# A byte limit on the transfers under way, and a weight folding in 14 TensorE groups instead of 26

## The chip, the cores and the metric

The kernel runs on one core of a Trainium2 chip. The metric is the time of one execution in device microseconds (us), the median of three runs. Five engines work side by side, each through its own instructions in order: TensorE (PE; its weight loads are shown as PEld), VectorE (DVE), ScalarE (ACT), GpSimd (POOL) and SyncE (SP). SP issues nearly all transfers of this kernel. An engine waits on semaphores for what another engine or a transfer has to deliver.

## The reference

There are 32 graphs of 512 nodes with 128 features each, `x` (32, 512, 128), and one symmetric 0/1 adjacency matrix per graph, `adj` (32, 512, 512). Four layers follow each other. Each normalises `x` over the features, takes the positive part `h`, and adds the layer's result to `x`:

```
h = jnp.maximum(_layernorm(x, axis=-1), 0.0); x = x + layer(h, adj, ...)
```

- Layer 0 is masked attention: q, k and v are each relu(h W + b), then a softmax of q k over the neighbours, times v.
- Layer 1 is a graph convolution whose weight matrix, one per graph, comes from an LSTM of 128 steps. It runs over a convolution of the last 128 nodes. The steps depend on each other, all 32 graphs advance together.
- Layer 2 is four sublayers, with 1, 1, 2 and 3 blocks of 128 input features. Each is

```
src_agg = einsum('bjv,bij->biv', nodes @ ws + bs, _l2norm(adj, 2))
dst_agg = einsum('bjv,bji->biv', nodes @ wd + bd, _l2norm(adj, 1))
upd = concatenate([src_agg, nodes @ wn + bn, dst_agg], axis=2)
out = tanh(upd @ wu + bu)
```

- Layer 3 is a graph convolution with a PReLU.

Because `adj` is symmetric, the two aggregations of a sublayer of layer 2 are with the same matrix. So `wu` can be multiplied into `ws`, `wd` and `wn` beforehand: `ws wu[0] + wd wu[2]` is one matrix that is applied before the aggregation, `wn wu[1]` another that is applied to the nodes themselves. The biases fold in the same way: `bs wu[0] + bd wu[2]` becomes a row, `bn wu[1] + bu` a column. This is the "folding" that the change edits. It is done once per call, for the four sublayers.

## The kernel before

**Recorded operations and a planner.** The function `symmetric` doesn't issue instructions. It records operations by the helpers `PE`, `ACT`, `DVE`, `POOL` and `DMA` (L853), each with an estimated duration, a rank, and the tiles that it reads and writes. One operation is one group: the instructions inside it stay together on the engine. `Plan.run` (L599) then simulates the engines with these estimates, takes what can start first and among those the lower rank, and gives out buffers (PSUM banks under the tag "mm", SBUF tiles under tags such as "ar", "gs", "x"). The result is one order per engine, which is issued at L754. Transfers stand in SP's order as the planner put them. A transfer has `gap`, the time that the planner expects from the end of its issue to its landing: 2.0 us by default, 3.8 (`LANDED`) for the loads of pass 2. The planner also charges `SWITCH` when PE changes between operations marked `tiled` (quarters of 32 columns) and others.

**Stages.** `pass_1` (L1116) runs over the 32 graphs: it loads `x` (f_x), normalises, makes queries, keys and values, stores keys and values (f_dkq, f_dv) to a scratch area in HBM, completes layer 0 for the last 128 nodes and makes the LSTM's inputs f_seq. `lstm` (L1210) makes the 128 steps, whose operations have the smallest ranks and so go first: matmuls f_z (L1224), then tanh on ACT (f_th), and products on DVE, ending in the write of f_seq (L1269) that the next step's f_z waits for. Between the steps of the LSTM the engines work on `pass_2` (L1279, ranks 20,000 and above). Per graph it loads f_h2 (192 KB), f_k2 (256), the adjacency matrix f_a (four tiles of 256, L1293), f_v2 (258), f_x2 (192 and 64). It then finishes layer 0 with the tiled matmuls f_pq, f_s and f_po (L1306, L1315, L1324), stores f_dx (L1335), and, for the first 22 graphs, squares the adjacency on ACT (f_ar, L1363), forms the first aggregation of layer 1 (f_pg, L1409, not tiled) and stores it (f_dgT, L1351). `rest` (L1423, ranks 30,000 and above) does the remaining layers graph by graph after the LSTM.

**The folding.** `fold(i, FOLD)` (L982) is called for the four sublayers behind graphs 4, 7, 10 and 13 of pass 2. It uses these groups on PE. Per block of 128 input features: three transposes of weights (f_wT, L998) and three matmuls (f_pw, L1005 to L1007), 7 blocks in all. Per sublayer: three transposes of bias rows (f_bT, L1014), two matmuls of them with `wu` (f_pb, L1021, L1022), and one matmul for the column (f_pc, L1026). That is 2 x 7 + 3 x 4 = 26. The bias rows come as three loads f_rowb (L986), each of one row of 512 bytes copied into all 128 partitions (64 KB). The weights come as one load f_w2 (L988) of 384, 384, 576 or 768 KB. Each f_wT and f_bT is copied to SBUF by ACT, and each f_pw by ACT into f_wf; DVE writes the folded bias row (L942) and the folded column (f_bcol).

Of the kernel before, what the change touches and what calls it, by code (L numbers as in the profile page):

```python
# [8 lines left out]
FP = mybir.dt.float32  # L9
# [4 lines left out]
P = 128  # L14
# [3 lines left out]
L2_CHUNKS = (1, 1, 2, 3)  # L18
# [14 lines left out]
C_Q, C_K, C_N, C_U = 0, 1, 2, 6  # L33
N_C = 9
R_V, R_CONV, R_SD, R_U3, R_L3 = 0, 1, 2, 10, 11
# [453 lines left out]
W_F = [0, 1, 2, 4]  # L489
# [26 lines left out]


class Op:
    __slots__ = ("engines", "rank", "no", "deps", "cells", "waits", "ready", "end", "engine", "start", "next", "gap", "tiled", "patience")


class Plan:
# [22 lines left out]
    def __init__(self, bufs, fifo, banks):  # L545
        self.banks = banks
        self.last = float("inf")
        self.soon = 0.0
        self.spared = float("inf")
        self.left = 0  # L550
        self.sealed = 0
        self.kept = ("mm", "gs",)
        self.ops = []
        self.bufs = bufs
        self.made = {}
        self.fifo = {t: [] for t in fifo}
# [12 lines left out]
    def op(self, engines, rank, reads=(), writes=(), after=(), gap=0.0, tiled=False):  # L569

        o = Op()
        o.engines, o.rank, o.no, o.gap = engines, rank, len(self.ops), gap
        o.tiled = tiled
        o.patience = 0.15
        deps = set(after)
        cells = []
        for acc, is_write in [(a, False) for a in reads] + [(a, True) for a in writes]:
            c, part = acc if isinstance(acc, tuple) else (acc, None)
            if c not in cells:
                cells.append(c)  # L580
            for key, (ws, rs) in c.parts.items():
                if part is None or key is None or key == part:
                    deps.update(ws)
                    if is_write:
                        deps.update(rs)
            mine = c.parts.setdefault(part, ([], []))
            if is_write:
                c.parts[part] = ([o], [])
            else:
                mine[1].append(o)  # L590
        deps.discard(o)
        o.deps = list(deps)
        o.cells = [c for c in cells if c.pool is not None]
        for c in o.cells:
            c.left += 1
        self.ops.append(o)
        return o

    def run(self, tc, queues):  # L599
        import bisect  # L600
# [14 lines left out]
        for o in ops:  # L615
            if o.rank >= self.last:
                k, sub = divmod(o.rank - self.last, 10)
# [71 lines left out]
        tiled = False  # L689
        by_rank = sorted((o for o in ops if o.rank >= 10_000 and o not in apart), key=lambda o: -o.rank)  # L690
        while done < len(ops):
            best = None
            for e, cands in pools.items():
                first = None
                held = expected.get(e)
                for rank, no, o in cands:
                    r = room(o)
# [22 lines left out]
            s, e, o = best  # L720
# [6 lines left out]
            if e == "PE":  # L727
                tiled = o.tiled
# [22 lines left out]
            done += 1  # L751
        self.order = order
        order.sort(key=lambda o: (o.start, o.no))
        with tc.manual_schedule(engines=queues):  # L754
            for o in order:
                o.engines[o.engine][1]()


def symmetric(ctx, tc, x, adj, weights, cols, rows, lstm_b, prelu_a, out, fail):
# [12 lines left out]
    nc = tc.nc  # L772
# [13 lines left out]
    SOON = 9_950.0  # L786
    LANDED = 3.8
    STORED = 5.0
    PATIENCE = 0.9
# [5 lines left out]
    const = ctx.enter_context(tc.tile_pool(name="f_const", bufs=1))  # L795
# [9 lines left out]
    plan = Plan(BUFS, ("ar", "x", "inv", "n0", "n1", "n2", "n3", "a"), "mm")  # L805
# [24 lines left out]
    T_TR = 0.11  # L830
# [7 lines left out]
    def t_dma(kb):  # L838
        return 0.1 + kb / 315.0

    def PE(rank, t, fn, r=(), w=(), **k):
        return plan.op({"PE": (t, fn)}, rank, r, w, **k)

    def ACT(rank, t, fn, r=(), w=(), **k):
        return plan.op({"ACT": (t, fn)}, rank, r, w, **k)

    def DVE(rank, t, fn, r=(), w=(), **k):
        return plan.op({"DVE": (t, fn)}, rank, r, w, **k)
# [2 lines left out]
        return plan.op({"POOL": (t, fn)}, rank, r, w, **k)  # L851

    def DMA(rank, kb, fn, r=(), w=(), **k):  # L853
        return plan.op({"SP": (max(0.45, t_dma(kb)), fn)}, rank, r, w, gap=k.pop("gap", 2.0), **k)

    def turn_tiles(dst, src):

# [22 lines left out]
    ident = const.tile([P, P], FP, name="f_ident")  # L880
# [27 lines left out]
    folded = plan.fixed(wf)  # L908
    bcols = plan.fixed(bcol)
    HEAD, LAST = 10_000, 19_000  # L910

    def load(rank, kb, dst, src):
        c = plan.fixed(dst)
        DMA(rank, kb, lambda: nc.sync.dma_start(dst, src), [], [c])
        return c
# [7 lines left out]
    for j in range(P // TURN):  # L923
        part = bass.ts(j, TURN)
        DMA(HEAD + 100, 4, lambda part=part: nc.sync.dma_start(
            lb[part], lstm_b.rearrange("s q f -> (s q) f")[:, part].partition_broadcast(TURN)), [], [(w_lb, j)])
    w_lstm = load(HEAD + 100, 512, w[:, W_IH : W_SD[0], :], weights[:, W_IH : W_SD[0], :])
    w_last = load(LAST, 64, w_fc, weights[:, W_FC, :])
    w_alpha = load(LAST, 1, alpha, prelu_a.partition_broadcast(P))
    POOL(LAST, 0.2, lambda: nc.gpsimd.tensor_scalar_mul(minus_alpha, alpha, -1.0), [], [w_alpha])  # L930
# [10 lines left out]
    def bias_row(rank, k, row, r):  # L941
        DVE(rank, t_dve(P), lambda: nc.vector.tensor_copy(brow[:, k, :], row()), r, [(biases, k)])  # L942
# [38 lines left out]

    def fold(i, FOLD):  # L982
        o = W_SD[i]
        rowb = new("ar", (P, 3, P), f"f_rowb_{i}")
        for k, r in enumerate((R_SD + 2 * i, R_SD + 2 * i + 1, R_U3)):
            DMA(FOLD, 64, lambda k=k, r=r: nc.sync.dma_start(rowb.t[:, k, :], rows[r].partition_broadcast(P)), [], [(rowb, k)])  # L986
        w2 = new("ar", (P, W_U[i] + 3 - o, P), f"f_w2_{i}")
        DMA(FOLD, 64 * (W_U[i] + 3 - o), lambda: nc.sync.dma_start(w2.t, weights[:, o : W_U[i] + 3, :]), [], [w2])  # L988

        def wu(k):  # L990
            return w2.t[:, W_U[i] - o + k, :]

        for c in range(L2_CHUNKS[i]):
            tp = bank(f"f_wT_{i}_{c}", (P, 3, P), whole=False)

            def turn(tp=tp, c=c):
                for k, m in enumerate((W_SD[i] + 2 * c, W_SD[i] + 2 * c + 1, W_N[i] + c)):
                    nc.tensor.transpose(tp.t[:, k, :], w2.t[:, m - o, :], ident)  # L998
            PE(FOLD, 3 * T_TR, turn, [w2], [tp])
            wt = new("gs", (P, 3, P), f"f_wTs_{i}_{c}")  # L1000
            ACT(FOLD, 0.5, lambda tp=tp, wt=wt: nc.scalar.copy(wt.t, tp.t), [tp], [wt])
            pw = bank(f"f_pw_{i}_{c}", (P, 2, P), whole=False)

            def mults(wt=wt, pw=pw):
                nc.tensor.matmul(pw.t[:, 0, :], wt.t[:, 0, :], wu(0), start=True, stop=False)  # L1005
                nc.tensor.matmul(pw.t[:, 0, :], wt.t[:, 1, :], wu(2), start=False, stop=True)
                nc.tensor.matmul(pw.t[:, 1, :], wt.t[:, 2, :], wu(1), start=True, stop=True)  # L1007
            PE(FOLD, 3 * t_mm(P), mults, [wt, w2], [pw])
            ACT(FOLD, 0.4, lambda pw=pw, c=c: nc.scalar.copy(wf[:, W_F[i] + c, :, :], pw.t), [pw], [(folded, (i, c))])
        bt_ps = bank(f"f_bT_{i}", (P, 3, P), whole=False)  # L1010

        def turn_b():
            for k in range(3):
                nc.tensor.transpose(bt_ps.t[:, k, :], rowb.t[:, k, :], ident)  # L1014
        PE(FOLD, 3 * T_TR, turn_b, [rowb], [bt_ps])
        bt = new("gs", (P, 3, P), f"f_bTs_{i}")
        ACT(FOLD, 0.5, lambda: nc.scalar.copy(bt.t, bt_ps.t), [bt_ps], [bt])
        pb = bank(f"f_pb_{i}", (P, P), whole=False)

        def mult_b():  # L1020
            nc.tensor.matmul(pb.t, bt.t[:, 0, :], wu(0), start=True, stop=False)  # L1021
            nc.tensor.matmul(pb.t, bt.t[:, 1, :], wu(2), start=False, stop=True)  # L1022
        PE(FOLD, 2 * t_mm(P), mult_b, [bt, w2], [pb])
        bias_row(FOLD, i, lambda: pb.t, [pb])
        pc = bank(f"f_pc_{i}", (P, 2), whole=False)
        PE(FOLD, 0.2, lambda: nc.tensor.matmul(pc.t[:, 0:1], wu(1), colb[:, C_N + i : C_N + i + 1], start=True, stop=True),  # L1026
           [w2, w_cols], [pc])
        DVE(FOLD, 0.2, lambda: nc.vector.tensor_add(bcol[:, i : i + 1], pc.t[:, 0:1],
                                                    colb[:, C_U + i : C_U + i + 1] if i < 3 else bt.t[:, 2, 0:1]),
            [pc, bt], [(bcols, i)])  # L1030


    def ln_stats(rank, xc, tiles, name, at=0):
# [576 lines left out]
    end = lstm()  # L1610
# [5 lines left out]
        rest(b, k, end)  # L1616
    counted()
    E = mybir.EngineType
    plan.last, plan.spared, plan.soon = 30_000, 20_000, SOON
    plan.run(tc, {E.PE, E.Activation, E.DVE, E.Pool, E.SP})  # L1620
    return flag[0]

# [81 lines left out]
```

## Time and profile before

| what | value |
|---|---|
| time, median of 3 runs | 1311.23 us (1306.88 to 1315.88) |
| time of the profiled execution | 1314.59 us |
| its span, first to last instruction | 1312.7 us |
| mean granted TensorE clock | 0.994 |
| moved by transfers | 232.82 MB, mean 177 GB/s |
| f_bT: median of one matmul | 273 ns (12) |
| f_pw: median of one matmul | 377, 275 and 275 ns (14 each) |
| ACT copies f_bTs | 4, median 487 ns |
| SP issue of one f_rowb | 428 ns median (12) |

The profile is of one execution, on the core that ran. "Busy" of PE is from the start of a matmul to its modelled end, so matmuls overlap in it, and an fp32 matmul appears as two entries. A group's line names source line, engine, operation, and "out<-in" tiles. The chain of waits is the work that ended last, followed back from the end step by step to what released it; "issue" in it is time in which an engine waited for nothing that the profile shows. In the table of waits, the three numbers are us in total, how often, and the longest. In the windows, each engine has its busy us and its instruction count, and the last three columns are the granted clock, the busy share of the 16 DMA engines and GB/s.

### The profile page before, as it was taken

To read this page: it belongs to the slowest core of one execution; us is meant where nothing else is said; L and a number is where in the kernel's file an instruction comes from. 1 tells how busy PE (TensorE), PEld (TensorE's weight loads), DVE (VectorE), ACT (ScalarE), POOL (GpSimd) and SP (SyncE) were. 2 spreads that over 40 slices of the span, in tenths; PEclk is the share of its full clock that TensorE was granted. 3 is DMA by queue.
4 is the path that set the end of the run, shared out by engine and by line. 5 is a ranking of instruction groups with operands and counts; after the bars stand their busy time and mean duration, and the time that the engine had idled before them with its cause. 6 is when DMAs were issued, how large, how long until landed. Compare 5 with 4: busy or idle time off the path is not lost.

```text
span 1312.7 us, 32944 instructions
## 1 busy us (share of the span) xinstructions
PE 1272.8 (97%) x12097; PEld 979.3 (75%) x12097; DVE 988.7 (75%) x3274; ACT 834.8 (64%) x2093; POOL 393.3 (30%) x733
## 2 busy tenths in 40 slices
PE   9999999999899999899999999999999999999996
PEld 6888866666567777677878778787787877877774
DVE  7999878778779887677667677676776787787654
ACT  5666667667678654577466666666666666675433
POOL 5655532112213233432213213132131332332000
PEclk9999999999899999999999999999999999999999
DMA  8888888847757867899377776777766465773311
GB/s 264 271 279 271 277 275 252 263 155 240 233 149 251 265 187 168 201 201 218 93 150 163 159 165 152 151 164 160 161 153 143 91 137 139 142 169 65 53 28 36
DMA packets 301259, 232.82 MB, mean 177 GB/s; under 512 B 139680, under 2 KB 246688, under 8 KB 301088
## 3 DMA queue, kind: packets, MB, share of 16 engines
q1 hardware_dynamic: 284192, 213.84, 59.4%
q0 software_dynamic: 16896, 16.78, 8.2%
q8 instruction: 98, 1.61, 0.5%
q14 instruction: 73, 0.60, 0.2%
HBM read 136.98 MB, written 62.13 MB: 152 GB/s over the span
## 4 chain that ended last, share of the span: by engine, by line
PE 85%; DVE 5%; ACT 3%; POOL 2%; DMA 2%; issue 2%; SPq 0%; ACTq 0%; DVEq 0%; POOLq 0%
PE f_pa L1409 17%; PE f_pa L1524 14%; PE f_py L1513 14%; PE f_pg L1409 9%; PE f_po L1324 5%; PE f_s L1315 5%; PE f_z L1224 4%; PE f_p L1565 2%; PE f_pol L1174 2%; PE f_pk L1131 2%; PE f_pv L1147 2%; PE f_pl L1467 2%; PE f_sl L1164 2%; PE f_pd L1199 1%; PE f_pq L1306 1%
## 5 line engine op out<-in xcount | busy, mean ns | idle before, releaser
L1409 PE MATMUL f_pa<-f_ar,f_y 128*128 128x512 f32 x1024 | 295.0, 426 | 2.1 <-ACT f_y L1392 2.1
L1409 PEld LDWEIGHTS f_pa<-f_ar,f_y 128*128 128x128 f32 x1024 | 189.3, 188 | 72.3 <-issue 35.8
L1513 PE MATMUL f_py<-f_wf,f_n 128*128 128x128 f32 x1280 | 173.5, 275 | 0.0
L1513 PEld LDWEIGHTS f_py<-f_wf,f_n 128*128 128x128 f32 x1280 | 164.4, 192 | 10.0 <-issue 1.9
L1524 PE MATMUL f_pa<-f_n,f_wf 128*128 128x512 f32 x320 | 152.9, 593 | 0.1
L1528 ACT ACTIVATE f_n<-f_pa,f_bcol 128x512 f32<-128x512 f32 x128 | 88.2, 689 | 93.6 <-PE f_pa L1524 93.4
L1363 ACT ACTIVATE f_ar<-f_a 128x512 fp32r<-128x512 f32 x216 | 133.7, 622 | 7.1 <-DMA f_a<-in_adj_dram 3.7
L1392 ACT CAST f_y<-f_py 128x512 fp32r<-128x512 f32 x128 | 74.8, 585 | 93.8 <-PE f_py L1513 90.7
L1481 POOL DMA_DIRECT2D f_das<-f_ar x32 | 27.9, 873 | 341.5 <-ACT f_ar L1363 267.9
L1324 PE MATMUL f_po<-f_v,f_e 128*32 128x129 f32 x3072 | 107.0, 274 | 7.5 <-issue 7.4
L1520 DVE TENSOR_TENSOR f_pa<-f_pa,f_inv 128x512 f32<-128x512 f32 x128 | 86.8, 694 | 27.7 <-PE f_pa L1409 27.4
L1324 PEld LDWEIGHTS f_po<-f_v,f_e 128*32 128x32 f32 x3072 | 90.4, 110 | 21.8 <-issue 15.2
L1393 DVE TENSOR_TENSOR f_y<-f_py,f_y 128x512 fp32r<-128x512 f32 x128 | 87.6, 685 | 24.1 <-ACT f_y L1392 23.8
L1315 PE MATMUL f_s<-f_q,f_k 128*32 128x384 f32 x1024 | 103.3, 490 | 0.6 <-issue 0.6
L1224 PE MATMUL f_z<-f_w,f_seq 128*32 128x128 f32 x2040 | 85.1, 277 | 8.6 <-DVE f_seq L1269 4.3
L1524 PEld LDWEIGHTS f_pa<-f_n,f_wf 128*128 128x128 f32 x320 | 57.5, 190 | 47.1 <-issue 37.8
L1224 PEld LDWEIGHTS f_z<-f_w,f_seq 128*32 128x32 f32 x2040 | 54.5, 109 | 45.1 <-ACT f_e L1318 8.7
L1486 DVE SCALAR_TENSOR_TENSOR f_junk<-f_a,f_aT 128x1024 bf16<-128x1024 f32 x64 | 78.1, 1220 | 5.7 <-DMA f_aT<-f_das 4.7
L1409 PE MATMUL f_pg<-f_ar,f_xp_d 128*128 128x512 f32 x256 | 75.2, 417 | 0.5 <-DVE f_lw L870 0.3
L1058 ACT ACTIVATE f_xn_c<-f_x,f_sh_c,f_rs_c 128x128 f32<-128x128 f32 x138 | 58.0, 486 | 24.2 <-DVE f_sh_c L1066 24.1
L1318 ACT ACTIVATE f_e<-f_s 128x384 f32<-128x384 f32 x128 | 60.7, 485 | 19.8 <-PE f_s L1315 14.8
L1513 PE MATMUL f_py<-f_wf,f_T_c 128*128 128x128 f32 x448 | 72.9, 275 | 0.0
(202 smaller groups left out, 2734.9 us busy)
## 6 DMA issues: line engine op xcount, KB each, us to landing
f_a<-in_adj_dram SPq DMA_DIRECT2D x30, 1024.0 KB
f_a<-in_adj_dram SPq DMA_DIRECT2D x96, 256.0 KB
f_das<-f_ar POOLq DMA_DIRECT2D x32, 512.0 KB, 4.8
f_dkq<-f_kh SPq DMA_DIRECT2D x32, 448.0 KB
f_dv<-f_v SPq DMA_DIRECT2D x32, 258.0 KB
f_v<-f_dv SPq DMA_DIRECT2D x32, 258.0 KB
f_x<-in_x_dram SPq DMA_DIRECT2D x32, 256.0 KB
f_al<-in_adj_dram SPq DMA_DIRECT2D x32, 256.0 KB
```

Of the source, the lines that this page charges most:

```text
L1224: nc.tensor.matmul(z.t[part, k, :, :], h, w[:, m : m + 4, part], start=False, stop=True, skip_group_check=True)
L1315: PE(R, t_mm(NR), lambda s=s, j=j: quarters(lambda p: nc.tensor.matmul(s.t[p], keys.t[:, j * P + p.start : j * P + p.stop], q.t, start=Tru ...
L1324: PE(R, t_mm(P), lambda t=t, j=j: quarters(lambda p: nc.tensor.matmul(po.t[p, t, :], es[j].t[:, t * P + p.start : t * P + p.stop], v.t[:, ...
L1363: ACT(rank, 0.62, lambda t=t: nc.scalar.activation(ar.t[:, t, :], a.t[:, t, :], AF.Square, accum_out=deg.t[:, t : t + 1]), [(a, t)], [(ar, ...
L1392: ACT(rank, t_act(N), lambda: nc.scalar.copy(parts.t[:, :, 0, :], src.t), [src], [(parts, 0)])
L1393: DVE(rank, t_dve(N), lambda: nc.vector.tensor_sub(parts.t[:, :, 1, :], src.t, f32(parts.t[:, :, 0, :])), [src, (parts, 0)], [(parts, 1)])
L1409: nc.tensor.matmul(pg.t, parts.t[:, j, k, :], ar.t[:, j, :], start=(k == 0 and j == 0), stop=(k == 1 and j == NT - 1))
L1486: nc.vector.scalar_tensor_tensor(junk, flat(a.t[:, 2 * k : 2 * k + 2, :]), 1.0, flat(aT.t[:, 2 * k : 2 * k + 2, :]), OP.mult, OP.not_equal ...
L1513: nc.tensor.matmul(py.t[:, j, :], nodes[n].t[:, bass.ts(j, P)], wf[:, W_F[i] + c, 0, :], start=False, stop=(c == nch - 1), skip_group_chec ...
L1520: before = DVE(R, t_dve(N), lambda pa=pa: nc.vector.tensor_mul(pa.t, pa.t, inv_row.t), [inv_row], [pa])
L1524: nc.tensor.matmul(pa.t, wf[:, W_F[i] + c, 1, :], nodes[n].t, start=False, stop=(c == nch - 1), skip_group_check=True)
L1528: ACT(R, 0.57, lambda pa=pa, n=n, i=i: nc.scalar.activation(n.t, pa.t, AF.Tanh, bias=bcol[:, i : i + 1]), [pa], [n])
```

## The change

Two things are changed.

First, a limit. Each operation now has `kb`, the size that the helper `DMA` was given. When the orders are issued, `hold_back` looks back along SP's order. For an operation of a rank from 20,000 to below 30,000 it adds up its own size and those before it until the sum would exceed 768 KB, and makes it wait until the transfer at which that happens has landed. The planner's simulation doesn't know of it. Before, SP's transfers were limited only by the eight semaphores that they use in turn.

```
+    def hold_back(self, tc, flight, o):
+        if not self.spared <= o.rank < self.last:
+            return
+        kb = 0
+        for ins, more in reversed(flight):
+            if kb + more > self.in_flight:
+                tc.add_manual_dep(flight[-1][0], ins.name, mybir.DependencyInfo(
+                    mybir.DependencyClass.Sync, mybir.DependencyReason.DATA), reason="transfers under way")
+                return
+            kb += more
...
+        flight = []
         with tc.manual_schedule(engines=queues):
             for o in order:
-                o.engines[o.engine][1]()
+                made = o.engines[o.engine][1]()
+                if o.engine == "SP":
+                    flight.append((made.ins, o.kb))
+                    self.hold_back(tc, flight, o)
...
-    plan.last, plan.spared, plan.soon = 30_000, 20_000, SOON
+    plan.last, plan.spared, plan.soon, plan.in_flight = 30_000, 20_000, SOON, 768
```

Second, the folding. The bias rows are no longer loaded as rows and transposed. One load at the start, f_sd_col, brings the nine bias vectors as columns (128 partitions x 9), element by element. As a stationary operand, a column is repeated 128 times by a stride of zero. The two bias matmuls and the column's matmul write into the same PSUM bank as the last block's f_pw, in the same group. The groups are then 7 of transposes and 7 of products, 14. The planner may let the product groups wait (`patience` 0.9 in place of 0.15) where they would reach into the expected start of an LSTM operation.

```
+    sd_col = const.tile([P, R_U3 + 1 - R_SD], FP, name="f_sd_col")
+    sd_cols = load(HEAD + 100, 5, sd_col, rows[R_SD : R_U3 + 1].rearrange("r p -> p r"))
...
-        rowb = new("ar", (P, 3, P), f"f_rowb_{i}")
-        for k, r in enumerate((R_SD + 2 * i, R_SD + 2 * i + 1, R_U3)):
-            DMA(FOLD, 64, lambda k=k, r=r: nc.sync.dma_start(rowb.t[:, k, :], rows[r].partition_broadcast(P)), [], [(rowb, k)])
...
-        bt_ps = bank(f"f_bT_{i}", (P, 3, P), whole=False)
...
-        pb = bank(f"f_pb_{i}", (P, P), whole=False)
...
-        pc = bank(f"f_pc_{i}", (P, 2), whole=False)
...
+        def mult_b(pw):
+            for k in range(2):
+                nc.tensor.matmul(pw.t[:, 2, :], sd_col[:, 2 * i + k : 2 * i + k + 1].to_broadcast([P, P]), wu(2 * k), start=k == 0, stop=k == 1)
+            nc.tensor.matmul(pw.t[:, 3, 0:1], wu(1), colb[:, C_N + i : C_N + i + 1], start=True, stop=True)
+        for c in range(nch):
+            last = c == nch - 1
+            pw = bank(f"f_pw_{i}_{c}", (P, 4, P), whole=False)
+
+            def both(c=c, pw=pw, last=last):
+                mults(c, pw)
+                if last:
+                    mult_b(pw)
+            PE(FOLD, (6 if last else 3) * t_mm(P), both, [wts[c], w2] + ([sd_cols, w_cols] if last else []), [pw]).patience = PATIENCE
+            ACT(FOLD, 0.4, lambda pw=pw, c=c: nc.scalar.copy(wf[:, W_F[i] + c, :, :], pw.t[:, 0:2, :]), [pw], [(folded, (i, c))])
+        bias_row(FOLD, i, lambda: pw.t[:, 2, :], [pw])
```

Since the planner works from the recorded operations, the orders of all engines are computed anew.

More of the change, by code (lines that the diff above doesn't have):

```diff
@@ L518 @@
 class Op:
-    __slots__ = ("engines", "rank", "no", "deps", "cells", "waits", "ready", "end", "engine", "start", "next", "gap", "tiled", "patience")
+    __slots__ = ("engines", "rank", "no", "deps", "cells", "waits", "ready", "end", "engine", "start", "next", "gap", "tiled", "patience", "kb")
 class Plan:
@@ L548, in __init__ @@
         self.soon = 0.0
+        self.in_flight = float("inf")
         self.spared = float("inf")
@@ L574, in op @@
         o.patience = 0.15
+        o.kb = 0
         deps = set(after)
@@ L853, in DMA @@
     def DMA(rank, kb, fn, r=(), w=(), **k):
-        return plan.op({"SP": (max(0.45, t_dma(kb)), fn)}, rank, r, w, gap=k.pop("gap", 2.0), **k)
+        o = plan.op({"SP": (max(0.45, t_dma(kb)), fn)}, rank, r, w, gap=k.pop("gap", 2.0), **k)
+        o.kb = kb
+        return o
     def turn_tiles(dst, src):
@@ L983, in fold @@
         o = W_SD[i]
-        rowb = new("ar", (P, 3, P), f"f_rowb_{i}")
-        for k, r in enumerate((R_SD + 2 * i, R_SD + 2 * i + 1, R_U3)):
-            DMA(FOLD, 64, lambda k=k, r=r: nc.sync.dma_start(rowb.t[:, k, :], rows[r].partition_broadcast(P)), [], [(rowb, k)])
+        nch = L2_CHUNKS[i]
         w2 = new("ar", (P, W_U[i] + 3 - o, P), f"f_w2_{i}")
@@ L991, in wu @@
             return w2.t[:, W_U[i] - o + k, :]
-        for c in range(L2_CHUNKS[i]):
+        wts = []
+        for c in range(nch):
             tp = bank(f"f_wT_{i}_{c}", (P, 3, P), whole=False)
+            wt = new("gs", (P, 3, P), f"f_wTs_{i}_{c}")
+            wts.append(wt)
             def turn(tp=tp, c=c):
@@ L999, in fold @@
             PE(FOLD, 3 * T_TR, turn, [w2], [tp])
-            wt = new("gs", (P, 3, P), f"f_wTs_{i}_{c}")
             ACT(FOLD, 0.5, lambda tp=tp, wt=wt: nc.scalar.copy(wt.t, tp.t), [tp], [wt])
[L1002 to L1007, printed above, removed]
@@ L1008, in fold @@
-            PE(FOLD, 3 * t_mm(P), mults, [wt, w2], [pw])
-            ACT(FOLD, 0.4, lambda pw=pw, c=c: nc.scalar.copy(wf[:, W_F[i] + c, :, :], pw.t), [pw], [(folded, (i, c))])
-        bt_ps = bank(f"f_bT_{i}", (P, 3, P), whole=False)
[L1012 to L1017, printed above, removed]
@@ L1018, in fold @@
-        pb = bank(f"f_pb_{i}", (P, P), whole=False)
[L1020 to L1024, printed above, removed]
-        pc = bank(f"f_pc_{i}", (P, 2), whole=False)
-        PE(FOLD, 0.2, lambda: nc.tensor.matmul(pc.t[:, 0:1], wu(1), colb[:, C_N + i : C_N + i + 1], start=True, stop=True),
-           [w2, w_cols], [pc])
@@ L1028, in fold, with mults @@
-        DVE(FOLD, 0.2, lambda: nc.vector.tensor_add(bcol[:, i : i + 1], pc.t[:, 0:1],
-                                                    colb[:, C_U + i : C_U + i + 1] if i < 3 else bt.t[:, 2, 0:1]),
-            [pc, bt], [(bcols, i)])
+        def mults(c, pw):
+            nc.tensor.matmul(pw.t[:, 0, :], wts[c].t[:, 0, :], wu(0), start=True, stop=False)
+            nc.tensor.matmul(pw.t[:, 0, :], wts[c].t[:, 1, :], wu(2), start=False, stop=True)
+            nc.tensor.matmul(pw.t[:, 1, :], wts[c].t[:, 2, :], wu(1), start=True, stop=True)
@@ new lines, in mult_b @@
+        def mult_b(pw):
+            for k in range(2):
+                nc.tensor.matmul(pw.t[:, 2, :], sd_col[:, 2 * i + k : 2 * i + k + 1].to_broadcast([P, P]), wu(2 * k), start=k == 0, stop=k == 1)
+            nc.tensor.matmul(pw.t[:, 3, 0:1], wu(1), colb[:, C_N + i : C_N + i + 1], start=True, stop=True)
+        for c in range(nch):
+            last = c == nch - 1
[6 more added lines that the diff above has]
+            ACT(FOLD, 0.4, lambda pw=pw, c=c: nc.scalar.copy(wf[:, W_F[i] + c, :, :], pw.t[:, 0:2, :]), [pw], [(folded, (i, c))])
@@ L1033, in ln_stats @@
+        bias_row(FOLD, i, lambda: pw.t[:, 2, :], [pw])
+        DVE(FOLD, 0.2, lambda: nc.vector.tensor_add(bcol[:, i : i + 1], pw.t[:, 3, 0:1],
+                                                    colb[:, C_U + i : C_U + i + 1] if i < 3 else sd_col[:, 8:9]),
+            [pw, sd_cols], [(bcols, i)])
     def ln_stats(rank, xc, tiles, name, at=0):
```

## The prediction

> **What bounds the kernel now.** I read the engine table first, then the chain of waits, then busy time stage by stage, with the stages cut where the LSTM's matmuls f_z begin (183.7) and end (501.8).
>
> ```profile
> PE 1272.8 (97%) x12097; PEld 979.3 (75%) x12097; DVE 988.7 (75%) x3274; ACT 834.8 (64%) x2093; POOL 393.3 (30%) x733
> PE 85%; DVE 5%; ACT 3%; POOL 2%; DMA 2%; issue 2%; SPq 0%; ACTq 0%; DVEq 0%; POOLq 0%
> ```
>
> ```profile
> core 0: us, PE busy (x) PEld busy (x) DVE busy (x) ACT busy (x) POOL busy (x), PEclk, DMA share, GB/s
> 0.00:183.70 183.70, 179.59 (x1444) 149.20 (x1444) 157.81 (x692) 114.18 (x231) 93.49 (x248) 1.00 0.86 272
> 183.70:501.80 318.10, 300.36 (x6149) 212.26 (x6150) 256.84 (x1078) 223.28 (x795) 84.87 (x159) 0.99 0.71 223
> 501.80:600.00 98.20, 90.58 (x730) 70.97 (x729) 67.28 (x199) 62.74 (x149) 34.15 (x53) 0.98 0.88 200
> 600.00:1312.70 712.70, 702.27 (x3778) 546.83 (x3776) 506.77 (x1307) 434.59 (x921) 180.80 (x275) 1.00 0.60 130
> ```
>
> TensorE sets the end everywhere. From 600 on it is full (in every 50 us window up to 1250 at least 49.9 busy), and nothing there is edited. What can be won lies in its idle time: 17.7 us in the LSTM stage (318.10 - 300.36) and 7.6 in the stage after it. All edits act in or before the LSTM stage, where an idle PE also holds up the LSTM's next step, because its queue is in order.
>
> Next, who ends PE's waits, and the chain at the long ones:
>
> ```profile
> PE f_po L1324 <- issue: 7.4, 5, 3.7
> PE f_pc L1026 <- DMA f_w<-in_weights_dram: 1.5, 1, 1.5
> ```
>
> ```profile
> 330.14 3.70 issue
> ...
> 462.31 2.35 issue
> ```
>
> "issue" means that no semaphore held PE. I looked for what else starts at these moments, in the DMA queues:
>
> ```profile
> q8 instruction: 98, 1.61, 0.5%
> ```
>
> 98 packets of 16 KB are 256 instructions of 64 bytes each, and 98 x 256 is about PE's stream (24,194 matmuls and loads): these are PE's instruction fetches. In the packet records one starts at 331.61 (the wait ended at 333.84) and one at 462.41 (ended 464.65). Counting PE instructions begun before the n-th fetch starts, less 256n, gives about 170 in the steady stage, mostly 200 to 385 in the LSTM stage, and 449, the largest of all, at exactly these two. So **PE ran out of instructions**: the fetch came late. Taking 165 as the point of request, and the landing of each SP transfer from the updates of its semaphore, the fetch started after 1.6 us on average with under 400 KB of SP transfers unlanded, 2.9 with 400 to 800, and 3.9 above (32 fetches). At 329.4 some 1540 KB were under way.
>
> **What the Trainium skill says.** "Runtime: NRT & Kernel Launch", section "Instruction fetch mechanics": instructions are streamed in 16 KiB blocks over a DMA queue that the sequencer drives while it executes, and this is mostly hidden. The trace agrees on the block; twice here it isn't hidden (3.70 and 2.35 us). "DMA: Bandwidth & Descriptors", section "Queues, rings and completion order": an SDMA engine takes turns between queues packet by packet. A backlog on SP's queue should then cost a fetch little; the trace shows 1.6 against 3.9 us, and I go by it. "TensorEngine Tiling (Array Packing)", section "Key Properties": a change of tiling mode drains the array. The trace has its price:
>
> ```profile
> 191.42 0.65 PE L1224 MATMUL f_z<-f_w,f_seq 128*32 128x128 f32 x16
> 192.00 2.11 PE L1409 MATMUL f_pg<-f_ar,f_xp_c 128*128 128x512 f32 x8
> 194.04 0.64 PE L1224 MATMUL f_z<-f_w,f_seq 128*32 128x128 f32 x16
> ```
>
> f_z to f_pg is 0.58 from start to start, where f_z to another tiled group is 0.44 (189.05 to 189.49): +0.14. The eight f_pg take 2.04 until the next f_z, while eight such matmuls in the steady stage take 1.84 (3.68 for 16 at 546.73): +0.20. A round trip costs 0.34 us.
>
> **The change part by part**, on the profiled execution's own time, 1314.6 (span 1312.7 and 1.9 around it). That is 3.4 above the median 1311.2.
>
> (a) The limit keeps SP's backlog at 768 KB. The two late fetches started 5.8 and 6.3 us after request 165, and PE used up the 284 instructions up to 449 in 4.3 and 6.2. With 2.9, the mean of the 400 to 800 KB class, the first comes 2.9 earlier and still leaves 0.8 of its wait, the second leaves nothing: 2.9 + 2.35 = **-5.25**. Ends: -8.1 (all issue waits of f_po and f_z) to 0. With them goes part of the clock loss behind: the f_pg at 353.96 took 3.43 in place of 2.04 in a window with clock 0.93. I take **-1.0** (0 to -1.4), since a 1.82 us wait on the LSTM at 351.5 helped to cause it.
>
> (b) The limit's own price: a wait on SP. Behind a held load stand the other loads of the batch and the stores f_dx and f_dgT; squares on ACT (L1363) wait for f_a, f_s for the keys, f_po for f_v. Transfers land in order, at 366 to 403 GB/s when many are queued:
>
> ```profile
> 327.00:328.00 1.00, 1.00 (x41) 1.00 (x41) 1.00 (x4) 0.45 (x3) 0.72 (x1) 1.00 0.64 58
> ...
> 331.00:332.00 1.00, 0.00 (x0) 0.00 (x0) 0.96 (x6) 0.00 (x0) 0.36 (x2) 1.00 1.10 403
> ```
>
> With 448 to 642 KB ahead they landed 1.86 to 2.25 us after issue (300.47, 246.43, 246.80, 320.58). So 768 KB per 2.25 us gives 350 GB/s, above the 250 to 276 of the busiest 25 us windows. A burst of one batch (192 + 256 + 4x256 + 258 + 192 + 64 KB, with stores 2.4 MB) takes 7.1 us in place of 6.2 at 400. Two oddities make it worse: 258 + 256 + 256 is 770, so a value load lets only two go, and the last fold's 768 KB waits for an empty queue and is waited for alone, some 4 us of SP. Against that, slack from landing to first use in the LSTM stage: f_a mostly 1.5 to 6 us, keys 3 to 50, values 6 to 60. Most delays are covered; I take **+2.5** (0 to +8; without cover each of some 22 early batches would pay 0.9).
>
> (c) Twelve f_rowb broadcasts go: SP 12 x 0.43 issue, beside. Their data is slow: at 327 to 328 the queue moved 58 GB/s (above) while f_rowb was in it, and one landed 2.8 us after the transfer before it, at 254.89 and at 330.04 alike. The fold weights behind them made PE wait 1.46 (second line of the waits). They come earlier now, but the planner still reckons 2.0 from issue to landing where they took 3.9 to 5.9: **-0.7** (-1.5 to +4, if PE stands at a transpose before its weights).
>
> (d) Groups. On PE the two built programs alternate between tiled and untiled matmuls 79 and 58 times from the first to the last f_z: 21 fewer, 10.5 round trips x 0.34 = 3.6. Twelve transposes go at 0.11 each (a group of four occupies PE 0.44 until the next starts): 1.3. Eight f_pb and four f_pc stay, inside f_pw. One added mark matmul for f_z, 0.2, is within the rounding. Of 4.9 I count **-3.5** (0 to -4.9), for in this stage some of it falls into waits on the LSTM. ACT loses four copies of 0.487, beside PE's work; should the LSTM's tanh stand behind one, it gains no more than 0.5 each, in the range. DVE keeps its eight operations.
>
> (e) f_sd_col: one load of 9 columns, at about 44 us. The skill's DMA page, "Rules for kernel authors", says one descriptor per element: 1152. The trace has no such load; its nearest are f_colb's 36-byte packets at 11 ns, so 1152 x 11 / 16 = 0.8 us. If reads of one small region crawl as f_rowb's did (some 160 packets per us from 250.0 to 252.4), up to 7. Slack of the x loads near (44 to 49): 1.6 and 3.2. **+0.5** (0 to +4).
>
> (f) The plan is recomputed, so all engines' orders shift. Work between first and last f_z is alike (f_po 1340 to 1296, f_s 460 to 480, f_pg 160 to 152), so I take 0, with +-4 for the 7.6 us idle after the LSTM.
>
> Sum: -5.25 - 1.0 + 2.5 - 0.7 - 3.5 + 0.5 = -7.45, that is 1307.2 by the profiled execution and, with 3.4 less, **1304** by the median.
>
> **The rivals.**
> Nothing visible (about 1310): the fetches are late for another reason, or another wait takes their place, the LSTM's own chain first. For: PE waits on f_seq stand second in the list (4.3 us). Then only (d) pays, -3.5, and (b) takes 2.5 back.
> Slower (about 1325): the limit starves the adjacency loads. It decides where landings come later than the slack of 1.5 to 3.6 us that half of the early batches have; an ACT square that waits blocks the LSTM's tanh behind it. 22 batches x 1 us = +22, less 8 from the other parts. Against it: 350 GB/s against 276 needed.
> A larger gain (about 1296): all 8.1 of issue, all 4.9 of groups, the 1.5, the clock's 1.0, and a limit for nothing: -15.5.
> That the limit does nothing is excluded: several SP loads now wait for two DMA semaphores where one stood.
>
> **How the numbers follow.** Forecast 0.57 (its own range 1297 to 1311), nothing visible 0.20, larger gain 0.11, slower 0.12. A measurement of this kernel tells about 1% from no change: below 1298.1 is faster, above 1324.3 slower. Faster: the larger gain and a quarter of the forecast, 0.26. Slower 0.12, same 0.62. Range 1293 to 1318.
>
> **What would show it.** Right: no issue wait over 1 us on PE before 502, fetch counts under 449, the LSTM's last f_z near 493, fewer idle us than 17.7. (c): no wait of f_pw or f_wT on f_w over 1 us. (b) wrong: ACT waiting for f_a in sum over 8 us, DMA under 200 GB/s from 184 to 500. (e) wrong: bn_stats late after 45 us and the first f_z past 186. The forecast falls if the LSTM stage is not shorter, or if the stage from 502 to 600 grows by what it gives.

## The result, and the profile after

The changed kernel takes 1371.07 us in the median of 4 runs (1364.19 to 1376.71), the kernel before in runs beside it 1310.95 (1306.88 to 1315.88). The ratio is 1.0455, with a 95% interval from 1.0391 to 1.0518. The prediction, 1304 in a range of 1293 to 1318, was wrong in sign and by 67 us.

The profiled execution took 1373.6, with a span of 1371.7, where the kernel before had 1312.7. Its page, engine table and chain of waits:

```profile
PE 1288.8 (94%) x12086; PEld 983.1 (72%) x12086; DVE 991.0 (72%) x3273; ACT 832.6 (61%) x2090; POOL 391.5 (29%) x733
...
PE 72%; DMA 16%; DVE 5%; ACT 3%; issue 1%; POOL 1%; SPq 1%; ACTq 0%; POOLq 0%; DVEq 0%
```

Instruction counts and busy times hardly differ, but for 16 us more of busy PE. PE's share of the chain fell from 85% to 72%, and transfers rose from 2% to 16%. Now the stages. As in the prediction, the LSTM stage is cut where the first f_z begins and 1.8 us behind the end of the last one, which comes at 552.7 (in the kernel before at 500.0, not at 501.8 as the prediction has it):

```profile
core 0: us, PE busy (x) PEld busy (x) DVE busy (x) ACT busy (x) POOL busy (x), PEclk, DMA share, GB/s
0.00:186.20 186.20, 179.23 (x1412) 148.68 (x1416) 153.36 (x684) 115.07 (x229) 96.11 (x248) 1.00 0.83 259
186.20:554.50 368.30, 312.15 (x6084) 212.40 (x6080) 254.07 (x1058) 224.74 (x799) 83.08 (x156) 0.94 0.62 186
554.50:652.00 97.50, 91.03 (x807) 71.66 (x807) 72.36 (x218) 58.17 (x140) 32.69 (x56) 0.98 0.95 228
652.00:1371.70 719.70, 706.41 (x3790) 550.38 (x3789) 511.18 (x1314) 434.66 (x922) 179.60 (x275) 0.99 0.59 129
```

The LSTM stage is where the loss is: 368.3 us in place of 318.1, with 56.2 us of idle PE (368.30 - 312.15) in place of 17.7, and 186 GB/s in place of 223. The granted clock fell there from 0.99 to 0.94, and about the same work shows more busy time (312 in place of 300). In the clock records of this stage there are nine stretches at half clock, each of 3.4 or 6.8 us and together 41 us; before there were two of 3.4. In the 3.4 us ahead of each of these eleven PE had been idle for at least 1.7. Not every such wait was followed by one. The waits from 180 to 560 us of the kernel after, first SP's own queue, then the other engines:

```profile
SPq L1317 <- DMA f_a<-in_adj_dram: 31.6, 18, 3.6
SPq L1310 <- DMA f_a<-in_adj_dram: 24.2, 27, 1.8
```

```profile
ACT f_ar L1380 <- DMA f_a<-in_adj_dram: 27.6, 18, 6.0
...
PE f_z L1241 <- DVE f_seq L1286: 24.1, 23, 5.1
...
DVE f_x L1072 <- DMA f_dx<-f_x: 18.5, 7, 5.0
ACT f_x L1075 <- DMA f_dx<-f_x: 17.1, 7, 5.5
```

L1310 issues the adjacency tiles, L1317 the value load behind them. Neither wait was among the twelve longest of SP before; the value load's line, then L1300, waited for a free buffer (21.5 us, for f_po). ACT, which squares the adjacency (L1380, before L1363), waits for tiles, and the LSTM behind it: PE waits 24.1 us for f_seq, before 4.3.

The last two lines show a second path. For the first 22 graphs layer 1 writes its normalised `x` over the tile f_x, and so has to wait until f_dx has been stored from it. Before, no wait for f_dx stands in this list. In that kernel SP issued the 26 stores f_dx of the stage 0.1 us in the mean after the last write of an f_x. In the kernel after it is 4.6 us: a store is held, or stands in SP's order behind what is held. ACT idled 17.1 us for their landing, DVE 18.5, and both engines also do the LSTM's work.

On the two pages, first of before, then of after, with the idle time ahead of the squares and what ended it:

```profile
L1363 ACT ACTIVATE f_ar<-f_a 128x512 fp32r<-128x512 f32 x216 | 133.7, 622 | 7.1 <-DMA f_a<-in_adj_dram 3.7
```

```profile
L1380 ACT ACTIVATE f_ar<-f_a 128x512 fp32r<-128x512 f32 x216 | 133.8, 622 | 43.3 <-DMA f_a<-in_adj_dram 40.2
```

How one such wait goes is in the chain of the kernel after (start, us, what):

```profile
195.65 4.88 DMA f_a<-in_adj_dram
...
200.56 0.72 ACT f_ar L1380 x2
201.28 0.15 ACT f_th L1267
...
202.64 5.26 DMA f_dx<-f_x
...
207.91 0.02 SPq L1310
...
207.96 2.66 DMA f_a<-in_adj_dram
...
210.64 0.72 ACT f_ar L1380 x2
211.37 0.14 ACT f_th L1267
```

A square waits for a late tile and the LSTM's tanh (L1267) stands behind the square on ACT. At 207.91 SP issues the next tile only because f_dx has just landed, and that tile needs 2.66 us more although only 448 KB are ahead of it. DVE's normalisation (L1072), with the LSTM's products behind it, began at 207.92, after 2.67 us of waiting for the same store. The transfers of these 21 us (195 to 216) as 40 slices of the transfer table, busy share in tenths and GB/s, in the kernel before and in the kernel after:

```profile
DMA  8399997995779819698726999897797679797899
GB/s 328 137 351 261 300 227 277 324 300 146 135 168 329 345 76 338 108 261 266 238 69 189 355 375 293 269 375 219 265 353 264 209 215 257 263 345 162 285 304 339
```

```profile
DMA  9779888974000388986798600027989489810010
GB/s 370 195 133 332 332 250 304 156 257 180 27 23 0 39 114 329 340 279 236 108 280 268 222 23 23 20 47 257 328 347 382 148 254 351 316 39 8 20 43 4
```

Before, the queue doesn't fall dry in these 21 us. After, it runs near 300 GB/s until what was let go has been moved, and then stands nearly still for 2 us and more (slices 11 to 14, 24 to 27, 36 to 40) until a landing is known to SP and the next transfer has begun.

### The profile page after: what moved, and what is told of

Read it like the earlier page. It is cut to its first block, busy times and chain, and to the rows that moved or that the text cites. A ratio compares the mean times of both kernels' runs of the same rounds, so it can differ in the third digit from the quotient of the medians.

```text
span 1371.7 us, 32913 instructions
## 1 busy us (share of the span) xinstructions
PE 1288.8 (94%) x12086; PEld 983.1 (72%) x12086; DVE 991.0 (72%) x3273; ACT 832.6 (61%) x2090; POOL 391.5 (29%) x733
## 4 chain that ended last, share of the span: by engine, by line
PE 72%; DMA 16%; DVE 5%; ACT 3%; issue 1%; POOL 1%; SPq 1%; ACTq 0%; POOLq 0%; DVEq 0%
PE f_pa L1426 16%; PE f_py L1530 14%; PE f_pa L1541 14%; PE f_pg L1426 7%; DMA f_a<-in_adj_dram 6%; PE f_po L1341 3%; PE f_s L1332 2%; PE f_z L1241 2%; DMA f_dx<-f_x 2%; PE f_p L1582 2%; PE f_pl L1484 2%; PE f_pk L1148 2%; DMA f_x<-in_x_dram 1%; PE f_pv L1164 1%; PE f_sl L1181 1%
## 5 line engine op out<-in xcount | busy, mean ns | idle before, releaser
L1426 PE MATMUL f_pa<-f_ar,f_y 128*128 128x512 f32 x1024 | 298.2, 428 | 1.1 <-ACT f_y L1409 1.1
L1380 ACT ACTIVATE f_ar<-f_a 128x512 fp32r<-128x512 f32 x216 | 133.8, 622 | 43.3 <-DMA f_a<-in_adj_dram 40.2
L1241 PE MATMUL f_z<-f_w,f_seq 128*32 128x128 f32 x2040 | 87.0, 288 | 45.5 <-DVE f_seq L1286 24.1
L1341 PEld LDWEIGHTS f_po<-f_v,f_e 128*32 128x32 f32 x3072 | 93.0, 114 | 21.5 <-issue 9.9
L1410 DVE TENSOR_TENSOR f_y<-f_py,f_y 128x512 fp32r<-128x512 f32 x128 | 87.5, 685 | 17.8 <-ACT f_y L1409 17.5
```

What stands on the lines that cost most here:

```text
L1241: nc.tensor.matmul(z.t[part, k, :, :], h, w[:, m : m + 4, part], start=False, stop=True, skip_group_check=True)
L1341: PE(R, t_mm(P), lambda t=t, j=j: quarters(lambda p: nc.tensor.matmul(po.t[p, t, :], es[j].t[:, t * P + p.start : t * P + p.stop], v.t[:, ...
L1380: ACT(rank, 0.62, lambda t=t: nc.scalar.activation(ar.t[:, t, :], a.t[:, t, :], AF.Square, accum_out=deg.t[:, t : t + 1]), [(a, t)], [(ar, ...
L1410: DVE(rank, t_dve(N), lambda: nc.vector.tensor_sub(parts.t[:, :, 1, :], src.t, f32(parts.t[:, :, 0, :])), [src, (parts, 0)], [(parts, 1)])
L1426: nc.tensor.matmul(pg.t, parts.t[:, j, k, :], ar.t[:, j, :], start=(k == 0 and j == 0), stop=(k == 1 and j == NT - 1))
```

## The experiments

Two theories stood at first. **L**: the limit is the whole loss. **P** (the plan): the new folding or its new order has a part in it. The first four runs:

**The folding alone** (no limit):

```
-    plan.last, plan.spared, plan.soon, plan.in_flight = 30_000, 20_000, SOON, 768
+    plan.last, plan.spared, plan.soon = 30_000, 20_000, SOON
```

> The change without its limit: folding in 14 groups, with every engine's order exactly that of the changed kernel, and no held transfers. Theory L (the limit starves the LSTM stage of transfers and is the whole loss): 1300 to 1312 us, ratio to before 0.992 to 1.001; fetch waits of PE ('issue' over 1 us) come back, 4 to 8 us in sum; ACT waits for f_a under 10 us. Theory P (the new order, or the folding in it, costs a good part): above 1325 us, with the same long PE gaps in the LSTM stage as in the changed kernel.

Measured: 1305.89, ratio 0.9968 (0.9955 to 0.9982). The stage and PE's wait for instructions:

```profile
182.30:491.20 308.90, 293.92 (x6084) 203.84 (x6081) 252.24 (x1058) 223.39 (x797) 82.28 (x156) 1.00 0.69 218
```

```profile
PE f_po L1341 <- issue: 2.9, 4, 2.2
```

All engines have the order of the kernel after, and the stage takes 308.9 us with 15.0 us of idle PE, at a clock of 1.00. P is excluded. ACT waited 7.0 us for f_a, as expected; the instruction waits were fewer than expected, 2.2 us in those over 1 us and 3.5 in all. The kernel after needs 59.4 us more for this stage with the same orders: 41.2 are idle PE, 18.2 are longer busy time, for which the 41 us at half clock (20.5 at most) are enough.

**The limit alone**, on the order of the kernel before (the lines of hold_back and kb added to it, 768):

> The kernel before, its order untouched, with the limit of 768 KB alone. Theory L: 1360 to 1385 us, ACT waiting for f_a 30 us or more, DMA from 184 us to the LSTM's end near 190 GB/s. Theory P: under 1335 us.

Measured: 1368.73, ratio 1.0453 (1.0418 to 1.0488): the whole loss. DMA moved 196 GB/s in the stage. But not all of the instruction waits went, and ACT's waits for f_a are not what was expected: 17.1 us over the whole span, not 30 or more. From 180 to 560 us ACT waited longer for the stores f_dx:

```profile
PE f_po L1344 <- issue: 5.9, 5, 3.3
```

```profile
ACT f_x L1078 <- DMA f_dx<-f_x: 30.9, 12, 5.8
...
ACT f_ar L1383 <- DMA f_a<-in_adj_dram: 13.4, 16, 2.4
```

Together 44.3 us, as in the kernel after (17.1 + 27.6 = 44.7). So the loss doesn't hang on late tiles alone: which of the two waits is the longer differs between these two orders of work.

**Two other limits**, each the kernel after with one number changed:

```
-SOON, 768
+SOON, 784   (1536 in the other)
```

> The changed kernel with 784 KB in place of 768, so that a value load of 258 KB and two tiles of 256 KB (770 KB) may be under way together. If the loss comes from the narrow windows around the value loads (15 of 50 landing gaps of the changed kernel end at f_v): 1340 to 1352 us. If the round trip of every held transfer makes it (three transfers per 2.6 to 3 us): 1362 to 1372 us, little changed.

> The changed kernel with 1536 KB. Round trip theory: six tiles of 256 KB per 4 us is 390 GB/s, as much as the queue gives at its best, so the limit costs nothing: 1300 to 1312 us, as without it. If held transfers cost through the order of SP (a store that is waited for with little behind it under way) and not through their rate: 1320 us or more.

Measured: 784 gives 1355.87, ratio 1.0348 (1.0317 to 1.0379), between the two expectations; 1536 gives 1305.86, ratio 0.9967 (0.9954 to 0.9980), as without a limit. So 16 KB more, which let 258 + 256 + 256 = 770 KB go together, are worth 1.07%, 14 us. SP's waits of 784 (180 to 560 us):

```profile
SPq L1310 <- DMA f_a<-in_adj_dram: 24.9, 28, 3.5
SPq L1317 <- DMA f_a<-in_adj_dram: 12.1, 15, 1.7
```

The tiles' own wait is the same, the value load's fell from 31.6 to 12.1. Most of that came back in the lines behind it (L1318, L1352 and L1368 wait 29.4 us for f_a, in the kernel after 13.0), so this view alone doesn't show where the 14 us were won.

**What sets the size.** I read the time from issue to landing of all transfers of 64 KB and more from 180 to 500 us of the kernel before, by what was under way with each:

| under way, itself included | transfers | mean us to landing | GB/s |
|---|---|---|---|
| 244 KB (alone) | 10 | 2.64 | 95 |
| 738 KB | 52 | 3.58 | 211 |
| 1017 KB | 63 | 4.00 | 260 |
| 1242 KB | 84 | 4.33 | 294 |
| 1564 KB | 78 | 4.95 | 323 |

The last column is an estimate, KB x 1.024 / us. In the kernel after, 206 transfers with 709 KB took 3.39, which gives 214 GB/s. The Trainium skill, "DMA: Bandwidth & Descriptors", section "Anatomy of one DMA — SWDGE (gpsimd) path", gives about 2.0 us fixed and the bytes at 436 GB/s for one transfer; it was fitted on single transfers that GpSimd issues. Used as an estimate for all that is under way on SP's queue, it gives 3.73 us for 738 KB and 2.57 for 244, near the measured 3.58 and 2.64, but 5.67 for 1564 KB, where 4.95 was measured. By the table a limit of 768 KB allows about 211 GB/s, less than the 223 that the stage moved before. The next runs test this **rate theory** on other limits.

> After with 1024 KB in place of 768. Rate theory (a transfer takes about 2.2 us plus 0.0017 us for each KB under way with it, so a limit caps the rate: 738 KB in 3.58 us is 206 GB/s, 1017 KB in 4.00 us is 254, 1564 KB in 4.95 us is 316, all from the landings of the kernel before): 254 covers the LSTM stage's mean of 223 but not its busiest windows of 250 to 276, so 1309 to 1318, ACT's waits for f_a between the 11 of 1536 and the 43 of 768. Rival, that only the narrow window around the 258 KB value loads costs (784 gave 15 back): with 1024 three tiles go beside a value load (258 + 3 x 256 is 1026, so it is only two) and the loss stays above 25, at 1330 to 1345.

> After with 1152 KB. Rate theory: 1152 KB in about 4.2 us is 274 GB/s, as much as the busiest windows need: 1304 to 1310, no more than 4 above the fold alone (1305.9). Rival, that any held load behind which stores and loads queue costs by itself, whatever the bytes: a limit that binds still often would leave 10 or more, 1316 and above.

(The rates in these texts count KB per us; in GB/s they are 2% higher.) Measured: 1024 gives 1322.35, ratio 1.0072 (1.0048 to 1.0095), and 1152 gives 1317.51, ratio 1.0034 (1.0016 to 1.0051); the kernel before ran at 1312.2 beside them, 2 higher than above. Both are above the rate theory's ranges, also with these 2 taken off. Against the folding alone (0.9968) that is +1.0% and +0.7%, 14 and 9 us, where the rate theory allowed up to 12 and 4. The limits come in the order that the theory says, and for 1024 its rival lies 8 us off. For 1152 the loss is about twice what the rate was to cost, and the time lies at the edge of the rival's range: a wait that binds may cost something by itself.

**What is held.** Transfers that count towards the limit but don't wait for it:

```
-                    self.hold_back(tc, flight, o)
+                    if o.adj:
+                        self.hold_back(tc, flight, o)
```

`adj` marks the loads f_a of pass 2; the second run has `if not o.adj`.

> After, where only the adjacency loads f_a of the second pass wait for the 768 KB limit; the other loads and the stores f_dx and f_dgT, which count towards it, no longer do. Rate theory (what counts is how many KB are under way on average): f_a is 88 of some 270 transfers of the stage, everything issued after a held f_a still stands behind it on SP's queue, and in between bursts of the others overshoot the limit: between the two ends, 1325 to 1350, f_a's waits on ACT still above 20. Rival, that the loss comes from stores and reloads through DRAM being held (f_dx and f_dgT stood with 28% in the chain of 198 to 250): freed here, at most 1318.

> After, where everything but the adjacency loads waits for the 768 KB limit. Rate theory: a burst of four or eight f_a (256 KB each) goes out at once, so far more than 768 KB is under way where the rate is needed most: 1308 to 1325, f_a's waits on ACT near the 11 of the 1536 KB limit. Rival, that held stores and reloads cost: still held here, 1345 or more.

Measured: 1326.55, ratio 1.0125 (1.0083 to 1.0168), and 1353.10, ratio 1.0321 (1.0279 to 1.0362). The first lies at the low end of the rate theory's range. The second misses it by 28 us and lies where the rival put it. The kernel with free adjacency loads still waits for them; its page, and SP's waits from 180 to 560 us:

```profile
L1382 ACT ACTIVATE f_ar<-f_a 128x512 fp32r<-128x512 f32 x216 | 133.8, 622 | 32.8 <-DMA f_a<-in_adj_dram 29.5
```

```profile
SPq L1319 <- DMA f_a<-in_adj_dram: 36.9, 19, 5.0
SPq L1370 <- DMA f_a<-in_adj_dram: 18.2, 6, 5.4
SPq L1354 <- DMA f_a<-in_adj_dram: 16.0, 9, 3.0
```

L1319 is the value load, L1354 and L1370 the stores. A burst of tiles fills the limit, the value load behind it waits up to 5.0 us for them to land, and the next graph's tiles, though not held, stand behind it on SP. Is it the stores? Two more runs mark f_dx and f_dgT of pass 2 in the same way (`if not o.store`, `if o.store`):

> After, where the stores f_dx and f_dgT of the second pass no longer wait for the 768 KB limit and all loads still do. Theory of one queue (a hold anywhere on SP delays everything behind it, and each held transfer pays its round trip of about 3.4 us before the next may go): loads are most of the transfers, so most of the loss stays, 1345 to 1368. Rival, that what costs is the held store with its reload through DRAM: 1325 or less.

> After, where only the stores f_dx and f_dgT of the second pass wait for the 768 KB limit and no load does. Theory of one queue: some 30 stores in the stage, each waiting until the burst of loads ahead of it has drained to 768 KB, and the next batch's loads behind it: 1308 to 1325. Rival, that held stores carry the loss: 1340 or more.

Measured: 1375.01, ratio 1.0464 (1.0411 to 1.0517), with loads held, even above the range given, and 1318.10, ratio 1.0047 (1.0031 to 1.0064), with stores held. The rival falls: freeing the stores gives nothing back, and holding them alone costs 0.8% against the folding alone. But freed stores aren't early ones. With only loads held, SP still issued f_dx 4.0 us in the mean after the last write of an f_x, because it stood behind a held load, and ACT idled 17.7 us for it (180 to 560). So these two runs clear the hold on the stores, not their lateness. Together:

| who waits for 768 KB | ratio | mean KB under way, 180 to 500 us | ACT idle for f_a, whole span | ACT idle for f_a and f_dx, 180 to 560 us | idle PE, first to last matmul |
|---|---|---|---|---|---|
| nobody (folding alone) | 0.9968 | 872 | 7.0 | 4.7 | 25.9 |
| limit 1536 | 0.9967 | 860 | 8.2 | 5.4 | 26.6 |
| limit 1152 | 1.0034 | 799 | 17.6 | 15.5 | 33.2 |
| stores only | 1.0047 | 795 | 18.2 | 17.5 | 36.1 |
| f_a only | 1.0125 | 792 | 20.3 | 25.0 | 40.8 |
| limit 1024 | 1.0072 | 768 | 18.0 | 19.4 | 37.5 |
| all but f_a | 1.0321 | 711 | 29.5 | 34.0 | 60.9 |
| limit 784 | 1.0348 | 641 | 31.5 | 35.5 | 62.4 |
| all but the stores | 1.0464 | 652 | 46.8 | 50.7 | 75.4 |
| all (the kernel after) | 1.0455 | 627 | 40.2 | 44.7 | 72.8 |
| all, order of before (limit alone) | 1.0453 | 615 | 17.1 | 44.3 | 70.2 |

The fewer KB are under way, the longer it takes, with small exceptions (f_a only, all but the stores). A part of this is by definition, since the same bytes in a longer stage are fewer at a time. ACT's two waits taken together put the runs in the order of their times (the first two are equal within their intervals); with its wait for f_a alone, the limit on the order of before falls out. How much of the loss is the lower rate, and how much is the order on SP behind a held load, these runs don't separate.

**The parts of the folding**, each on the kernel before without a limit. Groups merged, bias rows still loaded and transposed:

```
-                nc.tensor.matmul(pw.t[:, 2, :], sd_col[:, 2 * i + k : 2 * i + k + 1].to_broadcast([P, P]), wu(2 * k), start=k == 0, stop=k == 1)
+                nc.tensor.matmul(pw.t[:, 2, :], bt.t[:, k, :], wu(2 * k), start=k == 0, stop=k == 1)
```

(against the folding alone, with f_rowb, f_bT and f_bTs as before), and bias columns with the groups f_pb and f_pc apart:

> Before with the fold's groups merged but its bias rows still loaded as broadcast rows, transposed and copied: 18 groups in place of 26, no limit. By the price of a change of tiling (0.17 each way): 64 alternations between tiled and untiled matmuls from the first to the last f_z in place of 78, so -2.4, ratio 0.9982. If the order of work, planned anew, is what moved the fold kernel by -4.1, this one lies anywhere from -4 to +4; if the row loads are what cost, at 0.

> Before with the bias columns loaded once and broadcast as loaded operands, the groups not merged (22), no limit. By the price of a change of tiling: 70 alternations in place of 78, -1.4, and 12 transposes of 0.11 less, -1.3, and the reloads of rows gone, -0.7: together -3.4, ratio 0.9974. If the new order of work is what counts, anywhere from -4 to +4; if the column load costs what I allowed for it, +0.5.

Measured: 1321.00, ratio 1.0058 (1.0041 to 1.0074), which is +7.6 us, and 1311.69, ratio 0.9992 (0.9974 to 1.0010), beside 1312.2 of the kernel before. The columns alone are thus worth 1 us, with the forecast of -3.4 at the edge of the interval. Merging the groups alone is slower, though it has 14 fewer alternations of tiling. The same 316 us of the LSTM stage in the kernel before and in this one:

```profile
184.80:500.50 315.70, 297.99 (x6105) 210.46 (x6099) 255.12 (x1072) 221.70 (x789) 83.07 (x159) 0.99 0.71 223
```

```profile
184.80:500.50 315.70, 292.74 (x6028) 204.31 (x6028) 253.55 (x1063) 219.55 (x788) 80.39 (x156) 0.99 0.69 215
```

The LSTM ends at the same time (last f_z at 500.0 and 499.0), but PE was idle 5.3 us more beside it, and that work is left for afterwards. Its f_z waited 11.3 us for f_seq, before 4.3. The two parts, +7.6 and -1.0, don't add up to the folding's -4.2. Each of the three kernels has an order planned anew, which fits that the order moves them by more than the edits; no run holds the order fixed while the groups change, so this isn't shown.

## Why the prediction was wrong

**(b), the limit's own price, is the step that failed**: "768 KB per 2.25 us gives 350 GB/s", and from it +2.5 (0 to +8). The runs give 59 us for the limit on the order of before (1.0453), and 64 between the folding alone and the kernel after (1.0455 - 0.9968 of 1310). The 2.25 us came from four landings at the short end of their class: three stores and a load of 64 KB. All 52 transfers of the kernel before with 448 to 642 KB ahead took 1.86 to 6.44 us, 3.58 in the mean, and none of the 11 adjacency tiles among them less than 2.94. With 3.58 the same sum gives 211 to 220 GB/s against 223 moved in the mean and 250 to 276 needed in the busiest windows, and the answer is the other way round. The first oddity named, 770 over 768, was real and worth 14 us. The second, the last folding's load alone, occurred (issued at 381.29 with nothing under way, landed at 385.50).

**The rival "slower"** had the mechanism, starved adjacency loads and an ACT square that blocks the tanh behind it, and said what speaks for it: a slack of 1.5 to 3.6 us. In the kernel after, half of the squares of the LSTM stage start within 2.1 us of their tile's landing, a quarter within 0.1; before, 7% within 2. It was sized at 1 us for each of 22 graphs, and put at 0.12, "Against it: 350 GB/s against 276 needed". It also saw only f_a late. Holding everything but f_a cost 3.5% against the folding alone, holding f_a alone 1.6%, and the waits for f_dx, whose tile is written again, are in no term of the prediction.

**(a), late instruction fetches**, -5.25: PE's issue waits over 0.3 us fell from 8.2 to 1.7 us in sum. But the link to SP's backlog isn't borne out. The limit alone left 5.9, with 3.3 of it at 495 with 640 KB under way, and the folding without any limit had 3.0. In that run the fetch delay doesn't follow the KB unlanded: 2.8 us under 400, 2.8 from 400 to 800, 2.6 above (49 fetches), where before gave 1.6, 2.9, 3.9. Still, all other runs with a limit under 1536 KB had only 0.4 to 2.5, and the kernels with none or with 1536 had 3.0 to 10.5, each in one profiled execution. How much is the limit, how much the slower pace of PE in a longer stage, and how much where a fetch falls in the order stays open. The clock didn't rise but fell, to 0.979, with more long waits of PE than before.

**(c), (d), (e)**, together -3.7: the folding alone gave -4.2 (-2.4 to -5.9). The sum fits, its terms don't, so that is luck. (d) priced fewer alternations, and the run with 14 fewer was slower, so no run confirms that price. (c) called the row loads slow; in the run with merged groups the twelve took 3.65 us in the mean, much as other transfers do. (e) is nothing: f_sd_col landed 4.8 us after its issue in the folding alone and the first f_z began at 182.4, before it 183.7.

**(f)**, 0 with +-4 for the new plan: too narrow. The groups run lies 10 us from what its parts were priced at.

**What would show it** named the failure rightly: ACT waits for f_a over 8 us (40.2) and under 200 GB/s from 184 to 500 us (196).

## What to carry to other kernels

A limit on the bytes under way caps the rate at bytes over the time from issue to landing, so take that time as the mean of all transfers of that class in the trace, not from the best ones. Compare the cap with the rate of the busiest windows, not of the whole stage, and check that the limit isn't a few KB short of a natural set of tiles. On one in-order queue a transfer that waits delays all behind it, of whatever kind. So it also delays a store whose tile is to be written again; look for such tiles before holding anything. Here the two fastest kernels are the folding without a limit (0.9968) and with one of 1536 KB (0.9967), so that limit adds nothing.

## What the runs showed of the hardware

- Ten transfers with nothing else under way, 244 KB in the mean, took 2.64 us to land; with 738 KB under way it was 3.58, with 1564 KB 4.95. By these figures about 1 MB has to be under way for 260 GB/s (estimate from 1017 KB in 4.00 us).
- In half-microsecond slices of the LSTM stage, those under 50 GB/s make 76 us after and 53 before; slices over 300 GB/s are 23% after, 35% before. From 195 to 216 us of the kernel after the slow ones stand where the next transfer waits for a landing. Stretches of 2 us and more are not particular to the limit: they make 39 us after, 41 before.
- PE's clock records show full or half clock. All eleven stretches at half clock in the LSTM stages of before and after followed at least 1.7 us of idle PE in the 3.4 us ahead of them.
- Nine columns of 128 values, fetched element by element, landed 4.4 to 4.8 us after issue with 1024 KB ahead of them (the folding alone and the kernel after), little more than the 4.00 to 4.33 us of the larger transfers in the table with about as much under way.
